# One transpose per score tile with keys in order, and another order of the first tokens, experts and projections

## The chip, the cores and the metric

The kernel runs on one core of a Trainium2 chip. The core has five engines that run side by side: TensorE (PE) for matrix products, VectorE (DVE), ScalarE (ACT), GpSimd (POOL), and SyncE (SP), which here only issues transfers. ACT and POOL issue transfers too. Sixteen DMA engines move the data. The metric is device time in microseconds (us), the median of several executions; one further execution is recorded instruction by instruction, and that record is the profile.

## The reference

The input x is four sequences (batches) of 512 tokens with 256 features, all in float32. Three blocks are added to it in turn:

```
x = x + 0.5 * ffn(layernorm(x))
x = x + attention(layernorm(x))
x = x + 0.5 * ffn(layernorm(x))

ffn(x):       logits = x @ router_w + router_b           # 8 experts
              w = softmax of the two largest logits, 0 for the rest
              h = silu(x @ expert_w[e] + expert_b[e])    # 256 x 256 each
              y = x + (sum over e of w[e] * h[e]) @ proj_w + proj_b
              return norm_w * y / rms(y)

attention(x): 16 query heads, 4 key and value heads, head size 128
              q, k with rotary positions, k scaled by a weight per head
              p = softmax(causal(q k^T / sqrt(128)))
              return concat(p v) @ wo^T
```

## The kernel before

**Tiles.** A batch of 512 tokens is four token tiles of 128. Everything stays in SBUF; weights are loaded once. The first ffn of batches 0 and 1 is computed densely: every token goes through all eight experts (`ffn_dense`, line 683, which calls `ffn_experts`, 303, per token tile and then `ffn_finish`, 514). One step of `ffn_experts` takes a pair of experts: PE multiplies into PSUM (311), DVE adds the bias (316), ACT applies Silu (318), and DVE adds the two weighted results to `acc` (322, 324). The other batches are routed: tokens are gathered by expert into slots, and each slot tile loads its expert's weights from a copy in DRAM (`slots_pair`, 458 to 493, tiles `wt`). The last batches of the last block are dense again. `ffn_route` (217) does layernorm, the transposes of the tokens, the logits and the choice of two experts; in the transposes (`transposed`, 203) ACT copies the first half out of PSUM, and for dense batches DVE copies the second (210).

**Attention.** A group is one batch and one key/value head with its four query heads, so there are 16 groups. `project` (700) computes the group's key and its four queries, each with rotary positions (`rope`, 543). The four token tiles of queries are split into three parts, `PARTS = ((0, 1), (2,), (3,))`, so there are 48 units of a group and a part. `attn_scores` (604) handles a unit. For each query tile t it takes four score tiles r; each has on its 128 partitions 32 query positions times 4 heads, and as columns the (4t + r + 1) × 32 keys that these positions may see. PE computes the scores (615), DVE adds the mask and takes the maximum (617), ACT the exponentials and sums (622), DVE the reciprocals (626), ACT scales (628).

Then the probabilities are turned so that keys lie on partitions. DVE's transpose turns blocks of 32 × 32 where they lie: partitions stay within their quarter of 32. A key index is 128 j + 32 c + i. The tile `turned` has the axes [partition, c, j, x], where x is head-in-quarter and query. Whole key tiles j are written by one transpose (632) that splits the columns into (j, c, i) and writes c outermost; the remaining one to three blocks by a second (637). Sixteen copies by DMA per unit (645), one for each quarter g of partitions and each c, move the block rows to partitions 32 c to 32 c + 31 of `prT`. The blocks that the causal mask leaves out are set to zero once at the start (727). `attn_values` (651) multiplies with v, and `attn_out` (668) with wo.

**Memory that is used twice.** Until attention starts, the three `turned` tiles (`places`, 86) hold the expert weights of the first dense ffn: the first two pairs of experts are in the tile of part 2, the third in that of part 0, the fourth in that of part 1 (`experts`, 93). So a part's scores can't be written before the experts that lie there are done with.

**Order.** The loads are issued at the top of the program on SP's queue, in the order of the lines: batch 0, the four pairs of experts with their biases, batch 1, the attention weights; some small ones on ACT's. An issue waits where the semaphore that it uses belongs to an earlier load that hasn't landed. After the start (lines 718 to 732) a loop over the 48 units runs at 784: it projects a later group's heads, scores unit n + 2, and multiplies unit n by the values; steps of the other ffn work are put between by hand, each at its place (738 to 773). The program text isn't yet the order on the engines: a scheduler with its own estimate of times (line 44) merges what is written into one order for each engine, and an engine then runs its list strictly in order.

Of the kernel before, what the change touches and what calls it, by code (L numbers as in the profile page):

```python
# [9 lines left out]
F32 = mybir.dt.float32  # L10
# [5 lines left out]
P = 128  # L16
B = 4
S = 512
D = 256
H = 16  # L20
KV = 4
G = H // KV
HD = 128
E = 8
# [3 lines left out]
BL = 32  # L28
# [20 lines left out]
def macaron(ctx: ExitStack, tc: tile.TileContext, x, wq, wk, wv, wo, key_weights, router_w, router_b,  # L49
# [26 lines left out]
    def load_x(b):  # L76
        nc.sync.dma_start(xs[b], x[b * S : (b + 1) * S, :].rearrange("(t p) d -> p t d", p=P))

    load_x(0)
    nc.scalar.dma_start(rw, router_w.rearrange("(c p) e -> p c e", p=P))  # L80
    nc.scalar.dma_start(rb, router_b.partition_broadcast(P))
    nc.scalar.dma_start(rmp, ramp.partition_broadcast(P))

    places = [
        const.tile([P, NB, sum(t + 1 for t in ts), G * BL], F32, tag=f"turned{i}", name=f"turned{i}")
        for i, ts in enumerate(PARTS)
    ]

    def experts(who):
        flat = [a.rearrange("p c j x -> p (c j x)") for a in places]
        ews = [
            r.rearrange("p (e c f) -> p e c f", e=2, c=NC)
            for r in (flat[2][:, : 4 * D], flat[2][:, 4 * D :], flat[0][:, : 4 * D], flat[1][:, : 4 * D])
        ]
        eb = work.tile([P, E, D], F32, tag="prT", name=f"eb_{who}")
        for j in range(4):  # L100
            e = 2 * j
            for c in range(NC):
                nc.sync.dma_start(
                    ews[j][:, :, c, :],
                    expert_w[e : e + 2, c * P : (c + 1) * P, :].rearrange("e p f -> p e f"),
                )
            nc.sync.dma_start(
                eb[:, e : e + 2, :].rearrange("p e f -> p (e f)"),
                expert_b[e : e + 2, :].rearrange("e f -> (e f)").partition_broadcast(P),
            )  # L110
        return ews, [eb[:, 2 * j : 2 * j + 2, :] for j in range(E // 2)]

    def experts_late():
# [14 lines left out]
            yield  # L128

    dense = {0: experts(0)}  # L130
    load_x(1)
    nc.scalar.dma_start(pw, proj_w.rearrange("(c p) f -> p c f", p=P))
    nc.scalar.dma_start(pb, proj_b.partition_broadcast(P))
    nc.scalar.dma_start(nw, norm_w.partition_broadcast(P))
# [68 lines left out]
    def transposed(xn, xnT, who, ts=range(NT), dense=False):  # L203
        some = slice(ts[0] * P, (ts[-1] + 1) * P)
        for c in range(NC):
            pt = psum.tile([P, S], F32, tag="pt", name=f"ptx_{who}_{c}")
            for t in ts:
                nc.tensor.transpose(pt[:, t * P : (t + 1) * P], xn[:, t, c * P : (c + 1) * P], ident)
            if c == 1 and dense:
                nc.vector.tensor_copy(xnT[c][:, some], pt[:, some])  # L210
            else:
                nc.scalar.copy(xnT[c][:, some], pt[:, some])
# [4 lines left out]
    def ffn_route(f, b, group=None, ts=range(NT), half=False):  # L217
# [13 lines left out]
                dense_routed[f, b] = xn, xnT, {}  # L231
            xn, xnT, fws = dense_routed[f, b]
        yield from layernorm(b, xn, who, ts)
        transposed(xn, xnT, who, ts, group is None)
        if group:
            rows = slice(k * P, (k + NT) * P)
            nc.gpsimd.dma_start(group.xn[rows, :].rearrange("(t p) d -> p t d", p=P), xn)
# [62 lines left out]
        for i, t in enumerate(ts):  # L300
            fws[t] = fw[:, i, :]

    def ffn_experts(f, b, t, routed, weights):
        _, xnT, fws = routed
        ews, ebs = weights
        who = f"f{f}_{b}_{t}"
        acc = work.tile([P, 2, D], F32, tag="ga", name=f"acc_{who}")[:, 0, :]
        for j in range(E // 2):
            ph = psum.tile([P, 2, D], F32, tag="sc", name=f"ph_{who}_{j}", bufs=3)
            for c in range(NC):  # L310
                nc.tensor.matmul(  # L311
                    ph, xnT[c][:, t * P : (t + 1) * P], ews[j][:, :, c, :],
                    start=(c == 0), stop=(c == NC - 1),
                )
            h = work.tile([P, 2, D], F32, tag="h", name=f"h_{who}_{j}")
            nc.vector.tensor_tensor(h, ph, ebs[j], ALU.add)  # L316
            s = work.tile([P, 2, D], F32, tag="tb", name=f"s_{who}_{j}", bufs=3)
            nc.scalar.activation(s, h, AF.Silu)  # L318
            for i in range(2):
                e = 2 * j + i  # L320
                if e == 0:
                    nc.vector.tensor_scalar_mul(acc, s[:, i, :], fws[t][:, 0:1])
                else:
                    nc.vector.scalar_tensor_tensor(acc, s[:, i, :], fws[t][:, e : e + 1], acc, ALU.mult, ALU.add)
        return acc
# [277 lines left out]

    def attn_scores(ts, part, qT, kT, who):
        turned = places[part]
        runs = sum(t + 1 for t in ts)
        first = 0
        for t in ts:
            nm = small.tile([P, NB], F32, tag="nm", name=f"nm_{who}_{t}")
            sums = small.tile([P, NB], F32, tag="sums", name=f"sums_{who}_{t}")  # L610
            prs = []
            for r in range(NB):
                n = (NB * t + r + 1) * BL
                ps = psum.tile([P, S], F32, tag="sc", name=f"ps_{who}_{t}_{r}", bufs=3)
                nc.tensor.matmul(ps[:, :n], qT[:, NB * t + r, :, :], kT[:, :n], start=True, stop=True)  # L615

                nc.vector.tensor_tensor_reduce(  # L617
                    out=ps[:, :n], in0=ps[:, :n], in1=mask[:, S - n :], scale=-1.0, scalar=-LOWEST,
                    op0=ALU.add, op1=ALU.min, accum_out=nm[:, r : r + 1],
                )  # L620
                pr = work.tile([P, S], F32, tag="pr", name=f"pr_{who}_{t}_{r}", bufs=5)
                nc.scalar.activation(  # L622
                    pr[:, :n], ps[:, :n], AF.Exp, bias=nm[:, r : r + 1], scale=-1.0, accum_out=sums[:, r : r + 1]
                )
                prs.append((n, pr))
            nc.vector.reciprocal(sums, sums)  # L626
            for r, (n, pr) in enumerate(prs):
                nc.scalar.mul(pr[:, :n], pr[:, :n], sums[:, r : r + 1])  # L628

                whole = n // P  # L630
                if whole:
                    nc.vector.transpose(  # L632
                        turned[:, :, first : first + whole, r * BL : (r + 1) * BL].rearrange("p c j q -> p j c q"),
                        pr[:, : whole * P].rearrange("p (j c i) -> p j c i", c=NB, i=BL),
                    )
                if whole * P < n:
                    nc.vector.transpose(
                        turned[:, : r + 1, first + t, r * BL : (r + 1) * BL],
                        pr[:, whole * P : n].rearrange("p (c i) -> p c i", i=BL),
                    )  # L640
            first += t + 1
        prT = work.tile([P, NB, NT * G * BL], F32, tag="prT", name=f"prT_{who}")
        for g in range(NB):
            for c in range(NB):
                nc.sync.dma_start(  # L645
                    prT[c * BL : (c + 1) * BL, g, : runs * P],
                    turned[g * BL : (g + 1) * BL, c, :, :].rearrange("p j x -> p (j x)"),
                )
        return prT

# [61 lines left out]
    def score(n):  # L712
        if n < len(units):
            g, ts = units[n]
            who = "_".join(str(i) for i in (*groups[g], ts[0]))
            prTs[n] = attn_scores(ts, PARTS.index(ts), qTs[g], kTs[g], who)

    dense_routed = {}
    at_once(ffn_route(0, 0))
    ffn_dense(0, 0, dense[0], ffn_route(0, 1))  # L720
    ffn_dense(0, 1, dense[0], attn_prepare(0))

    for turned, ts in zip(places, PARTS):
        first = 0
        for t in ts:
            for c in range(1, NB):
                nc.gpsimd.memset(turned[:, c, first + t, : c * BL], 0.0)
            first += t + 1
    project(0, range(G))
    score(0)  # L730
    project(1, (0, 1))
    score(1)


    PLACES = 4
# [116 lines left out]
```

## Time and profile before

| | us |
|---|---|
| median of three runs | 888.08 |
| lowest and highest run | 885.06 and 888.1 |
| the profiled execution | 882.37 |
| its span, first to last instruction | 880.7 |

The span is what the profile's times are measured in; the profiled execution is 1.7 us longer than its span. The profile's first page gives each engine's busy time. The chain that ended last is followed back from the last instruction, at each step to what released it, so its shares say what the end of the program hung on. A row of a timeline reads: start, length, engine, line, operation, what is written and read, how many instructions are merged, and in brackets how long the engine was idle before and what ended that. "SPq" and "ACTq" are the queues on which an engine issues transfers. The granted clock is the share of TensorE's full speed.

### The profile page before, as it was taken

To read this page: it belongs to the slowest core of one execution; us is meant where nothing else is said; L and a number is where in the kernel's file an instruction comes from. 1 tells how busy PE (TensorE), PEld (TensorE's weight loads), DVE (VectorE), ACT (ScalarE), POOL (GpSimd) and SP (SyncE) were. 2 spreads that over 40 slices of the span, in tenths; PEclk is the share of its full clock that TensorE was granted. 3 is DMA by queue.
4 is the path that set the end of the run, shared out by engine and by line. 5 is a ranking of instruction groups with operands and counts; after the bars stand their busy time and mean duration, and the time that the engine had idled before them with its cause. 6 is when DMAs were issued, how large, how long until landed. Compare 5 with 4: busy or idle time off the path is not lost.

```text
span 880.7 us, 11501 instructions
## 1 busy us (share of the span) xinstructions
PE 807.2 (92%) x2752; PEld 478.4 (54%) x2752; DVE 624.1 (71%) x1961; ACT 512.4 (58%) x1260; POOL 301.0 (34%) x402
## 2 busy tenths in 40 slices
PE   4899798999999898999989999999799979999995
PEld 2444344656466555565545556657566546645552
DVE  1889569786357677776387878447674788788795
ACT  1444359656547574686487766647664576673263
POOL 4123274213142217672312322242322765301222
PEclk9999999899999999999999999999999999999997
DMA  7900011335576655243213333466666334342000
GB/s 237 409 24 6 20 60 43 85 81 142 139 224 188 193 145 152 69 118 107 61 34 87 98 106 89 135 181 199 196 175 211 88 112 135 108 118 74 13 7 24
DMA packets 68979, 103.32 MB, mean 117 GB/s; under 512 B 16624, under 2 KB 47600, under 8 KB 68528
## 3 DMA queue, kind: packets, MB, share of 16 engines
q1 hardware_dynamic: 61744, 84.48, 32.5%
q0 software_dynamic: 6048, 17.57, 7.1%
q10 hardware_dynamic: 1120, 0.54, 0.2%
q8 instruction: 22, 0.36, 0.2%
q14 instruction: 45, 0.37, 0.1%
HBM read 45.11 MB, written 15.47 MB: 69 GB/s over the span
## 4 chain that ended last, share of the span: by engine, by line
PE 53%; SPq 13%; DVE 11%; DMA 9%; ACT 9%; issue 4%; POOL 1%; POOLq 0%; ACTq 0%; DVEq 0%
SPq L645 12%; PE pa L658 10%; PE pw L671 8%; PE ph_f L311 7%; PE pp_q L584 6%; PE ps L615 6%; DMA wt<-wb 3%; PE ph_f L337 3%; PE phg L485 3%; PE po_f L524 3%; ACT tb_q L553 3%; PE pp_k L584 2%; ACT pr L622 2%; PE pv_a L573 2%; ACT pr L628 2%
## 5 line engine op out<-in xcount | busy, mean ns | idle before, releaser
L622 ACT ACTIVATE pr<-ps,nm 128x32 f32<-128x32 f32 (+15 forms) x256 | 123.2, 485 | 76.6 <-DVE nm L617 66.2
L615 PE MATMUL ps<-kT,qT 128*128 128x160 f32 (+15 forms) x512 | 146.9, 408 | 13.0 <-ACT pr L622 12.5
L658 PE MATMUL pa<-prT,v_a 128*128 128x512 f32 x320 | 149.8, 596 | 2.8 <-DMA prT<-turned 1.1
L617 DVE CUSTOM_DVE_ANT_0 ps<-ps,mask 128x32 f32<-128x32 f32 (+15 forms) x256 | 110.5, 446 | 40.5 <-PE ps L615 38.8
L560 POOL TENSOR_TENSOR qT<-qT,tb_q 128x512 f32<-128x512 f32 x64 | 81.2, 1271 | 156.2 <-DVE tb_q L558 101.7
L584 PE MATMUL pp_q<-xnT_a,wq_sb 128*128 128x512 f32 x256 | 124.2, 615 | 4.4 <-DVE qT L557 1.8
L615 PEld LDWEIGHTS ps<-kT,qT 128*128 128x128 f32 x512 | 86.6, 191 | 69.5 <-issue 32.4
L671 PE MATMUL pw<-wo_sb,oT 128*128 128x256 f32 x512 | 122.0, 382 | 1.8 <-ACT oT L664 1.1
L628 ACT ACTIVATE pr<-pr,sums 128x32 f32<-128x32 f32 (+15 forms) x256 | 112.3, 511 | 12.7 <-DVE sums L626 12.2
L671 PEld LDWEIGHTS pw<-wo_sb,oT 128*128 128x128 f32 x512 | 96.9, 191 | 31.1 <-issue 13.3
L553 ACT ACTIVATE tb_q<-pp_q,kws 64x512 f32<-64x512 f32 x128 | 87.4, 683 | 30.8 <-PE pp_q L584 28.8
L632 DVE STREAM_TRANSPOSE turned<-pr 128x128 f32<-128x128 f32 (+3 forms) x208 | 93.1, 447 | 16.8 <-ACT pr L628 14.4
L658 PEld LDWEIGHTS pa<-prT,v_a 128*128 128x128 f32 x320 | 58.6, 190 | 58.4 <-issue 54.1
L584 PEld LDWEIGHTS pp_q<-xnT_a,wq_sb 128*128 128x128 f32 x256 | 48.6, 196 | 56.1 <-issue 44.5
L469 POOL DMA_INDIRECT xg<-xn_dram,source x46 | 44.9, 976 | 92.8 <-PE ptg L477 64.0
L557 DVE SCALAR_TENSOR_TENSOR qT<-pp_q,kws,cos_sb 128x512 f32<-128x512 f32 x64 | 47.8, 748 | 33.2 <-ACT tb_q L553 32.6
L311 PE MATMUL ph_f<-turned,xn_f 128*128 128x512 f32 x128 | 64.0, 652 | 5.3 <-DVE h_f L316 5.3
L664 ACT COPY oT<-pa 128x512 f32<-128x512 f32 x64 | 37.1, 580 | 32.4 <-PE pa L658 29.9
L318 ACT ACTIVATE s_f<-h_f 128x512 f32<-128x512 f32 x48 | 29.6, 628 | 43.8 <-DVE h_f L316 28.1
L558 DVE TENSOR_TENSOR tb_q<-tb_q,sin_sb 128x512 f32<-128x512 f32 x64 | 52.1, 815 | 0.3 <-ACT tb_q L553 0.3
L485 PE MATMUL phg<-wt,xT 128*128 128x256 f32 x184 | 46.0, 383 | 6.4 <-DMA wt<-wb 6.4
L622 ACT ACTIVATION_READ_ACCUMULATOR pr<-ps,nm 128x1 f32 x256 | 50.2, 196 | 0.0
(168 smaller groups left out, 1165.7 us busy)
## 6 DMA issues: line engine op xcount, KB each, us to landing
prT<-turned SPq DMA_DIRECT2D x512, 48.0 KB
wt<-wb SPq DMA_DIRECT2D x46, 384.0 KB
prT<-turned SPq DMA_DIRECT2D x256, 64.0 KB
rows<-hg SPq DMA_DIRECT2D x22, 256.0 KB
x<-in_x_dram SPq DMA_DIRECT2D x4, 512.0 KB
turned<-in_expert_w_dram SPq DMA_DIRECT2D x8, 256.0 KB
wq_sb<-in_wq_dram SPq DMA_DIRECT2D x1, 2048.0 KB
wo_sb<-in_wo_dram SPq DMA_DIRECT2D x1, 2048.0 KB
```

The source lines that it names most:

```text
L311: nc.tensor.matmul(ph, xnT[c][:, t * P : (t + 1) * P], ews[j][:, :, c, :], start=(c == 0), stop=(c == NC - 1),)
L553: nc.scalar.mul(tb[o, :], ps[i, :], scale[i, :])
L560: nc.gpsimd.tensor_tensor(dst, dst, blocks(tb), ALU.subtract)
L584: nc.tensor.matmul(ps, w[:, c, h * HD : (h + 1) * HD], xnT[:, c, :], start=(c == 0), stop=(c == NC - 1))
L615: nc.tensor.matmul(ps[:, :n], qT[:, NB * t + r, :, :], kT[:, :n], start=True, stop=True)
L617: nc.vector.tensor_tensor_reduce(out=ps[:, :n], in0=ps[:, :n], in1=mask[:, S - n :], scale=-1.0, scalar=-LOWEST, op0=ALU.add, op1=ALU.min, ...
L622: nc.scalar.activation(pr[:, :n], ps[:, :n], AF.Exp, bias=nm[:, r : r + 1], scale=-1.0, accum_out=sums[:, r : r + 1])
L628: nc.scalar.mul(pr[:, :n], pr[:, :n], sums[:, r : r + 1])
L632: nc.vector.transpose(turned[:, :, first : first + whole, r * BL : (r + 1) * BL].rearrange("p c j q -> p j c q"), pr[:, : whole * P].rearr ...
L645: nc.sync.dma_start(prT[c * BL : (c + 1) * BL, g, : runs * P], turned[g * BL : (g + 1) * BL, c, :, :].rearrange("p j x -> p (j x)"),)
L658: nc.tensor.matmul(po, v[:, j, kv * HD : (kv + 1) * HD], prT[:, :, (first + j) * P : (first + j + 1) * P], start=(j == 0), stop=(j == t),)
L671: nc.tensor.matmul(pw_, oT[:, i, :], wo_sb[:, kv * G + i, :], start=(i == 0), stop=(i == G - 1))
```

## The change

There are three edits.

1. `turned` now has the axes [partition, key block, x], with key block 4 j + c, in the order of the keys. Each score tile is turned by one transpose whatever its number of blocks. The copies take every fourth key block.
2. The first token tile of batch 0 is loaded and routed alone. The rest of batch 0 and batch 1 are loaded behind the first pair of experts, ahead of the other three pairs.
3. The dense ffn of batch 1 is written out: tiles 0 and 1 as before, the pairs of experts of tiles 2 and 3 in the order 2, 3, 0, 1, and between them batch 0's attention preparation and its first projections. The zeros of part 0 come before the first scores, the other parts' after them; the finish of tiles 2 and 3 stands behind the first scores and the first head of the second group.

Besides, in the last block the second half of the tokens' transposes is copied by ACT, as the first half is, and no longer by DVE.

```diff
-    load_x(0)
+    nc.sync.dma_start(xs[0][:, 0, :], x[:P, :])
...
-        const.tile([P, NB, sum(t + 1 for t in ts), G * BL], F32, tag=f"turned{i}", name=f"turned{i}")
+        const.tile([P, NB * sum(t + 1 for t in ts), G * BL], F32, tag=f"turned{i}", name=f"turned{i}")
...
+            if j == 0:
+                nc.sync.dma_start(xs[0][:, 1:, :], x[P:S, :].rearrange("(t p) d -> p t d", p=P))
+                load_x(1)
...
-    load_x(1)
...
-        transposed(xn, xnT, who, ts, group is None)
+        transposed(xn, xnT, who, ts, group is None and f == 0)
...
-                whole = n // P
-                if whole:
-                    nc.vector.transpose(
-                        turned[:, :, first : first + whole, r * BL : (r + 1) * BL].rearrange("p c j q -> p j c q"),
-                        pr[:, : whole * P].rearrange("p (j c i) -> p j c i", c=NB, i=BL),
-                    )
-                if whole * P < n:
-                    nc.vector.transpose(
-                        turned[:, : r + 1, first + t, r * BL : (r + 1) * BL],
-                        pr[:, whole * P : n].rearrange("p (c i) -> p c i", i=BL),
-                    )
+                nc.vector.transpose(
+                    turned[:, first : first + n // BL, r * BL : (r + 1) * BL],
+                    pr[:, :n].rearrange("p (k i) -> p k i", i=BL),
+                )
...
-                    prT[c * BL : (c + 1) * BL, g, : runs * P],
-                    turned[g * BL : (g + 1) * BL, c, :, :].rearrange("p j x -> p (j x)"),
+                    prT[c * BL : (c + 1) * BL, g, : runs * BL].rearrange("p (j x) -> p j x", x=G * BL),
+                    turned[g * BL : (g + 1) * BL, c:runs:NB, :],
...
-    at_once(ffn_route(0, 0))
+    at_once(ffn_route(0, 0, ts=(0,)))
+    at_once(ffn_route(0, 0, ts=(1, 2, 3)))
     ffn_dense(0, 0, dense[0], ffn_route(0, 1))
-    ffn_dense(0, 1, dense[0], attn_prepare(0))
...
+    acc0 = experts_of(0)
+    acc1 = experts_of(1)
+    finish(0, acc0)
+    at_once(attn_prepare(0))
+    acc2 = experts_of(2, (2, 3))
+    finish(1, acc1)
+    acc3 = experts_of(3, (2, 3))
+    project(0, (0,))
+    acc2 = experts_of(2, (0,), acc2)
+    project(0, (1,))
+    acc3 = experts_of(3, (0,), acc3)
+    project(0, (2,))
+    acc2 = experts_of(2, (1,), acc2)
+    project(0, (3,))
+    acc3 = experts_of(3, (1,), acc3)
+    zeros(0)
     score(0)
-    project(1, (0, 1))
+    finish(2, acc2)
+    project(1, (0,))
+    finish(3, acc3)
+    project(1, (1,))
+    zeros(1)
+    zeros(2)
     score(1)
```

Here `experts_of(t, pairs, acc)` is `ffn_experts` for batch 1, tile t, which now takes a list of pairs and a sum to go on from; `finish` is `ffn_finish` for that batch, and `zeros(part)` does the memsets of one part.

More of the change, by code (lines that the diff above doesn't have):

```diff
@@ L93, in experts @@
     def experts(who):
[L94 to L98, printed above, removed]
+        room = [places[2][:, :8, :], places[2][:, 8:, :], places[0][:, :8, :], places[1][:, :8, :]]
+        ews = [r.rearrange("p (e c h) x -> p e c (h x)", e=2, c=NC) for r in room]
         eb = work.tile([P, E, D], F32, tag="prT", name=f"eb_{who}")
@@ L301, in ffn_route, with ffn_experts @@
             fws[t] = fw[:, i, :]
-    def ffn_experts(f, b, t, routed, weights):
+    def ffn_experts(f, b, t, routed, weights, pairs=range(E // 2), acc=None):
         _, xnT, fws = routed
@@ L306, in ffn_experts @@
         who = f"f{f}_{b}_{t}"
-        acc = work.tile([P, 2, D], F32, tag="ga", name=f"acc_{who}")[:, 0, :]
-        for j in range(E // 2):
+        first = acc is None
+        if first:
+            acc = work.tile([P, 2, D], F32, tag="ga", name=f"acc_{who}")[:, 0, :]
+        for j in pairs:
             ph = psum.tile([P, 2, D], F32, tag="sc", name=f"ph_{who}_{j}", bufs=3)
@@ L320, in ffn_experts @@
                 e = 2 * j + i
-                if e == 0:
-                    nc.vector.tensor_scalar_mul(acc, s[:, i, :], fws[t][:, 0:1])
+                if first and e == 2 * pairs[0]:
+                    nc.vector.tensor_scalar_mul(acc, s[:, i, :], fws[t][:, e : e + 1])
                 else:
@@ L605, in attn_scores @@
         turned = places[part]
-        runs = sum(t + 1 for t in ts)
+        runs = NB * sum(t + 1 for t in ts)
         first = 0
@@ L628, in attn_scores @@
                 nc.scalar.mul(pr[:, :n], pr[:, :n], sums[:, r : r + 1])
-                whole = n // P
-                if whole:
-                    nc.vector.transpose(
-                        turned[:, :, first : first + whole, r * BL : (r + 1) * BL].rearrange("p c j q -> p j c q"),
-                        pr[:, : whole * P].rearrange("p (j c i) -> p j c i", c=NB, i=BL),
-                    )
-                if whole * P < n:
-                    nc.vector.transpose(
-                        turned[:, : r + 1, first + t, r * BL : (r + 1) * BL],
-                        pr[:, whole * P : n].rearrange("p (c i) -> p c i", i=BL),
-                    )
-            first += t + 1
+                nc.vector.transpose(
+                    turned[:, first : first + n // BL, r * BL : (r + 1) * BL],
+                    pr[:, :n].rearrange("p (k i) -> p k i", i=BL),
+                )
+            first += NB * (t + 1)
         prT = work.tile([P, NB, NT * G * BL], F32, tag="prT", name=f"prT_{who}")
@@ L718, in macaron, with experts_of, finish, zeros @@
     dense_routed = {}
-    at_once(ffn_route(0, 0))
+    at_once(ffn_route(0, 0, ts=(0,)))
+    at_once(ffn_route(0, 0, ts=(1, 2, 3)))
     ffn_dense(0, 0, dense[0], ffn_route(0, 1))
-    ffn_dense(0, 1, dense[0], attn_prepare(0))
-    for turned, ts in zip(places, PARTS):
+    routed = dense_routed.pop((0, 1))
+    def experts_of(t, pairs=range(E // 2), acc=None):
+        return ffn_experts(0, 1, t, routed, dense[0], pairs, acc)
+    def finish(t, acc):
+        at_once(ffn_finish(0, 1, t, routed[0][:, t, :], acc))
+    def zeros(part):
         first = 0
-        for t in ts:
+        for t in PARTS[part]:
             for c in range(1, NB):
-                nc.gpsimd.memset(turned[:, c, first + t, : c * BL], 0.0)
-            first += t + 1
-    project(0, range(G))
-    score(0)
-    project(1, (0, 1))
+                nc.gpsimd.memset(places[part][:, first + NB * t + c, : c * BL], 0.0)
+            first += NB * (t + 1)
+    acc0 = experts_of(0)
[14 more added lines that the diff above has]
+    zeros(0)
+    score(0)
+    finish(2, acc2)
[4 more added lines that the diff above has]
+    zeros(2)
     score(1)
```

## The prediction

> **What bounds the kernel now.** I read the first page (busy shares, the chain that ended last), then the time cut by stage, then what TensorE (PE) waits for, then the queue of SyncE (SP), because the chain names it.
>
> ```profile
> PE 807.2 (92%) x2752; PEld 478.4 (54%) x2752; DVE 624.1 (71%) x1961; ACT 512.4 (58%) x1260; POOL 301.0 (34%) x402
> PE 53%; SPq 13%; DVE 11%; DMA 9%; ACT 9%; issue 4%; POOL 1%; POOLq 0%; ACTq 0%; DVEq 0%
> ```
>
> PE carries the time, but the second owner of the chain is not VectorE (DVE): it is SP's queue, and nearly all of that (12% by line) is the issuing of the copies of line 645.
>
> ```profile
> 0.00:25.00 25.00, 11.47 (x38) 6.50 (x39) 6.53 (x25) 3.71 (x4) 9.36 (x37) 1.00 0.77 258
> 25.00:60.00 35.00, 34.59 (x99) 17.19 (x98) 31.21 (x95) 17.31 (x30) 7.59 (x13) 0.90 0.61 237
> 60.00:100.00 40.00, 37.78 (x104) 18.22 (x103) 28.58 (x76) 14.09 (x31) 10.45 (x22) 0.96 0.04 14
> 100.00:110.00 10.00, 4.12 (x15) 2.69 (x14) 7.46 (x18) 3.64 (x8) 3.71 (x7) 0.86 0.00 0
> 110.00:160.00 50.00, 44.24 (x134) 23.50 (x133) 40.28 (x122) 35.27 (x84) 28.38 (x34) 0.88 0.18 54
> 160.00:810.00 650.00, 616.31 (x2188) 378.58 (x2187) 456.08 (x1469) 410.68 (x1052) 224.38 (x258) 0.99 0.46 130
> ```
>
> Columns: stretch, length, busy PE, weight loads, DVE, ScalarE (ACT), POOL, then granted clock, DMA share, GB/s. Before 160 us PE is idle 27.8 us and its clock is below 1; in the 650 us after that it is idle 33.7 us at full clock. The start is where time lies loose. Two waits hold most of it:
>
> ```profile
> 22.35 1.08 DVE L192 BATCH_NORM_STATS2 st_f<-x 128x6 f32<-128x256 f32 x3 [10.63 <-DMA x<-in_x_dram]
> 24.46 5.83 PE L311 MATMUL ph_f<-turned,xn_f 128*128 128x512 f32 x9 [4.06 <-DVE h_f L316]
> 108.09 0.66 PE L518 MATMUL ptc_f<-ident,acc_f 128*128 128x128 f32 x2 [5.88 <-DVE acc_f L324]
> ```
>
> DVE stands 10.63 us before the statistics of batch 1, whose load comes last, and PE stands behind it. At 108 us PE waits 5.88 us for the last token tile's sum, with the projections queued behind. In the main stage, SP's queue:
>
> ```profile
> 454.67 90.90 SPq L645 DMA_DIRECT2D prT<-turned  x135
> L645 SPq DMA_DIRECT2D prT<-turned x768: 507/589/1952, 147.9 to 806.6; - x192
> L77 SPq DMA_DIRECT2D x<-in_x_dram x4: 368/406/449, 1.5 to 22.3; - x4
> L538 SPq DMA_DIRECT2D out_dram<-x x8: 332/332/519, 807.2 to 877.6; - x8
> L493 SPq DMA_DIRECT2D rows<-hg x24: 338/385/1460, 241.0 to 674.6; - x24
> ```
>
> 135 issues without a break in 90.9 us are 0.673 us each; the median issue is 0.589, and about 0.045 passes between two (the 16 of one unit, from 281.56, took 10.78 with one slow one of 1.31). So 0.634 is SP's floor, 10.15 us per unit of 16, and the units pass every 10.77. Between 460 and 540 us PE is busy 76.85 of 80, 10.3 us per unit: PE and SP are bound together there.
>
> **The change, part by part. (a) Transposes.** Their rows:
>
> ```profile
> L632 DVE STREAM_TRANSPOSE turned<-pr 128x384 f32<-128x384 f32 x64 | 35.7, 558 | 6.2 <-ACT pr L628 4.4 <-DMA prT<-turned 1.7
> L632 DVE STREAM_TRANSPOSE turned<-pr 128x256 f32<-128x256 f32 x64 | 27.5, 430 | 5.9 <-ACT pr L628 5.4 <-DMA prT<-turned 0.3
> L632 DVE STREAM_TRANSPOSE turned<-pr 128x128 f32<-128x128 f32 x64 | 19.0, 297 | 4.6 <-ACT pr L628 4.5
> L637 DVE STREAM_TRANSPOSE turned<-pr 128x96 f32<-128x96 f32 x64 | 15.5, 242 | 0.1
> L637 DVE STREAM_TRANSPOSE turned<-pr 128x64 f32<-128x64 f32 x64 | 13.5, 211 | 0.3
> L637 DVE STREAM_TRANSPOSE turned<-pr 128x32 f32<-128x32 f32 x64 | 11.5, 179 | 3.1 <-ACT pr L628 2.5 <-DMA prT<-turned 0.4
> ```
>
> 128 columns more cost 128 to 133 ns, so a fixed part of 150 to 170 ns stands in every instruction. Each score tile of the query tiles 1 to 3 whose keys don't fill whole tiles has two transposes: 3 × 3 × 16 groups = 144 pairs become one. 144 × 0.15 = 21.6 us off DVE. DVE isn't the bound: it holds 11% of the chain, 97 us, out of 624 busy; the same share of 21.6 is 3.4 us. I take −3.5; 0 if PE and SP cover it all, −8 if also the ps and pr handshake shortens (PE waits 9.2 us on ACT's pr in the main stage). The new form's stride is only longer; where it costs more per column than 1 ns no row shows, and a twentieth more on 134 us of transposes would be 6 us of DVE, under 1 on the chain.
>
> **(b) The copies of line 645.** Their number stays 768. The source of each was one run of 1.5 or 2 KB per partition; now it is three or four runs of 512 B, 96 or 128 pieces instead of 32. Nothing in this trace issues a copy from SBUF to SBUF in such pieces, so I bound it. Rows: 128 rows in one run each take 0.332 to issue (out), 256 pieces 0.385 (rows), 512 pieces 0.406 (x): more pieces and one dimension more cost 0.05 to 0.075. Lower end 0. The other end: the present copy already takes 0.257 more than out with a quarter of the rows, for a reason the trace doesn't show; if a dimension more costs that again, +0.257. I take +0.06, from the nearest count of pieces. SP's floor becomes 0.694, 11.1 us per unit. The stretches that SP fills without a break (from 159.99: 77 issues in 51.01; 454.67: 135 in 90.90; 720.39: 80 in 52.92; 775.50: 37 in 24.68) hold 20.6 units at 10.67. (11.1 − 10.67) × 20.6 = +9. The chain says the same: 12.4% of 880.7 is 109 us, 172 issues × 0.06 = +10. I take +9, from 0 to about +110 (below). What waits behind SP: the next unit's copies, the expert rows wt that PE waits for (6.4 us now), and so pa. On the 16 DMA engines the copies move the same 42 MB; their share is 0.46 in that stage, and I cost them at nothing; without that cover, 0.2 us more to landing on some ten copies that stand on the chain would be 2.
>
> A rule speaks against this part. The Trainium skill, Perfetto Trace Analysis, section What "DMA-bound" means, says that the window of an issuing sequencer is descriptor generation, and that large descriptors are what matter. If issue time went with the number of pieces, an issue would take 1.8 to 2.4 us and the stage would more than double; the rows above (512 pieces in 0.406) don't show that, so the rule moves no term here.
>
> **(c) First loads.** Now batch 1 lands behind 0.5 (batch 0) + 2 (weights) + 1 (biases) MB and ACT's 0.5, at 22.3 us. After the change only 0.13 + 0.77 + 0.38 MB of SP's stand before its 0.5, with ACT's 0.5 some 2.3 MB. The first 10 us move 1.67 MB, the next 10 go at 277 GB/s: about 12.3 us. The price: the other three pairs of experts wait behind 0.5 MB more, 1.8 us, the last landing near 20.6. DVE's stop is gone; late next are the weights. By 24.46 PE has done three expert steps (one step is four matmul records, 1.72 us in the chain). After, with token tile 0 finished at 22.3, it has done 5.2, that is 3.9 us gained; steps of other tiles drawn forward make 6.4 at most. Lower end 0: ACT issues pw, pb and nw, and each issue waits for an earlier load (at 3.03, 5.21, 7.39 now). If nw waits for batch 1, ACT's first copy goes from 10.81 to about 14. I take −4.5. The first tile routed alone adds some 15 small DVE instructions of 0.15 to 0.2 and at most two table loads of 1.28: 5.5 us, hidden by DVE's 6.5 busy of 25; uncovered they eat the gain.
>
> **(d) Experts between projections.** From 60 to 160 us PE is idle 13.9 us. The work doesn't shrink, it is put into these gaps: the 5.88 at 108 and half of the other 8 go. Next to bind is DVE: 76 us busy of these 100, 76 of 93 after. I take −7 (0 to −12). POOL's memsets now stand ahead of each score stage instead of in a block; 12 × 0.12 = 1.4 us, hidden by POOL's idle 7 of 10. The end of the dense stage, finish of tiles 2 and 3, is moved behind the first scores; only batch 0's own last steps need it.
>
> **(e) Clock.** (1 − 0.90) × 35 + 0.04 × 40 + 0.14 × 10 + 0.12 × 50 = 12.5 us of the start are lost to a lower clock, after the gaps. Two gaps fewer: −2 (0 to −4).
>
> **(f) The last block's copies from DVE to ACT:** three, 1 us, where DVE is busy 54 of the last 70: −0.5; ACT has room.
>
> Sum: −3.5 + 9 − 4.5 − 7 − 2 − 0.5 = −8.5. The profiled execution took 882.37 us (span 880.7, 1.7 around it): 873.9. The median of the runs is 888.08, 5.7 above; carried over, 879.6, said as 879.
>
> **Rivals.** *SP takes over* (slower). The 17.5 us of gains are used up when a unit takes 0.85 more on 20.6 units: 11.52 us, 0.72 per issue with its gap, so from +0.086 per issue on it is slower. At +0.15, (12.54 − 10.67) × 20.6 = 38, less 17.5: +21, 909. At +0.257, 14.26 a unit: +74, and in the 260 us with expert slots (some 18 units of 14 us) +2 each: 980. For it: the unbroken queue. Against it: the flat rows of issue time. *The start gives nothing*: DVE, busy 31.2 of 35 from 25 to 60, or ACT's queue becomes the bound there. −4 + 9 = +5: 893. For it: how full DVE is; against: 28 us of PE idle. *The copies cost SP nothing*: −17.5, with more from the start up to −28: 860 to 870.
>
> **How the numbers follow.** This forecast (own range 869 to 886) 0.47; SP takes over 0.23; the start gives nothing 0.15; copies free 0.15. Half a per cent, 4.4 us, is what a measurement can tell from no change. Faster: 0.82 of the forecast, all of the free case: 0.53. Same: 0.15, the rest of the forecast and part of the idle start. Slower 0.32. 864 to 912 leaves out the low tail of the free case and SP beyond +0.15, together under 2 in 10.
>
> **What would show it.** The issue of line 645: median 0.64 to 0.66 confirms (b), above 0.68 (0.72 with the gap) ends the forecast. 256 transposes, about 112 us. Batch 1's statistics near 12 us; no PE wait of several us near 108; PE idle before 160 near 15. It goes wrong if the order in which the engines get the new work puts a late load ahead of ready work, or SP's queue shows breaks, which would mean it was never the bound.

## The result, and the profile after

The changed kernel is slower: 890.2 us median (886.17 to 895.14) against 885.37 (878.92 to 889.11) for before on the same chip, a ratio of 1.0061 with a 95% interval of 1.0042 to 1.0081. The forecast of 879 us, 9 below the 888.08 that stood for before, went the wrong way, though the time lies within its range. The profiled execution took 888.89 us, its span 887.2, 6.5 more than that of before's profile.

The first page of the changed kernel, busy times and the chain by engine:

```profile
PE 807.6 (91%) x2752; PEld 480.2 (54%) x2752; DVE 626.2 (71%) x1833; ACT 515.6 (58%) x1268; POOL 304.1 (34%) x404
PE 51%; SPq 14%; DVE 14%; DMA 8%; ACT 7%; issue 4%; POOL 1%; POOLq 0%; DVEq 0%; ACTq 0%
```

The same stretches as in the prediction (length, busy PE, weight loads, DVE, ACT, POOL, then granted clock, DMA share, GB/s), of the changed kernel:

```profile
0.00:25.00 25.00, 14.63 (x41) 7.67 (x42) 12.39 (x56) 7.87 (x10) 11.51 (x42) 0.93 0.79 269
25.00:60.00 35.00, 33.02 (x108) 17.41 (x106) 29.33 (x92) 16.67 (x31) 8.32 (x14) 1.00 0.59 229
60.00:100.00 40.00, 39.43 (x100) 18.52 (x101) 32.51 (x80) 15.93 (x31) 13.07 (x24) 0.96 0.04 14
100.00:110.00 10.00, 5.82 (x15) 2.67 (x14) 8.55 (x14) 6.36 (x10) 3.72 (x3) 0.94 0.00 0
110.00:160.00 50.00, 43.14 (x155) 26.42 (x155) 41.66 (x142) 36.79 (x98) 26.91 (x39) 0.87 0.24 69
160.00:810.00 650.00, 606.53 (x2138) 372.75 (x2137) 443.92 (x1290) 402.37 (x1029) 223.43 (x252) 0.98 0.47 128
```

Before 160 us PE is idle 24.0 us instead of 27.8. In the 650 us after that it is idle 43.5 instead of 33.7, and the clock is a hundredth lower. So the start did gain, and the main stage lost more. Where the start's waits stood (start, length, engine, line, and in brackets the idle time before), batch 1's statistics and PE's wait near 108 us:

```profile
13.11 1.08 DVE L191 BATCH_NORM_STATS2 st_f<-x 128x6 f32<-128x256 f32 x3 [4.29 <-DMA x<-in_x_dram]
14.99 1.08 DVE L191 BATCH_NORM_STATS2 st_f<-x 128x6 f32<-128x256 f32 x3 [0.58 <-DMA x<-in_x_dram]
...
107.68 0.44 PE L519 MATMUL ptc_f<-ident,acc_f 128*128 128x128 f32 x2 [3.18 <-DVE acc_f L325]
```

DVE's stop of 10.63 us is now 4.29 (for the rest of batch 0) and 0.58; the 5.88 us at 108 are 3.18. The transposes (count, then busy time in us and mean in ns, then DVE's idle time before them) and the issue of the copies (count, then shortest/median/longest in ns, first and last start in us):

```profile
L630 DVE STREAM_TRANSPOSE turned<-pr 128x32 f32<-128x32 f32 (+15 forms) x256 | 108.7, 447 | 14.9 <-ACT pr L629 11.5
...
L638 SPq DMA_DIRECT2D prT<-turned x768: 305/598/1963, 135.3 to 810.5; - x192
```

The median issue grew by 9 ns, from 589 to 598, not by 60. The first copy is issued at 135.3 us, 12.6 earlier than before (147.9); the last at 810.5, 3.9 later (806.6). From first to last copy the main stage takes 675.2 us where before takes 658.7: 16.5 us are lost there. What loses them is the question of the experiments.

### The profile page after: what moved, and what is told of

Same layout as the page of the kernel before. It is cut to its first block, busy times and chain, and to the rows that moved or that the text cites. A ratio compares the mean times of both kernels' runs of the same rounds, so it can differ in the third digit from the quotient of the medians.

```text
span 887.2 us, 11351 instructions
## 1 busy us (share of the span) xinstructions
PE 807.6 (91%) x2752; PEld 480.2 (54%) x2752; DVE 626.2 (71%) x1833; ACT 515.6 (58%) x1268; POOL 304.1 (34%) x404
## 2 busy tenths in 40 slices
DMA packets 126338, 103.31 MB, mean 116 GB/s; under 512 B 16640, under 2 KB 113152, under 8 KB 125888
## 4 chain that ended last, share of the span: by engine, by line
PE 51%; SPq 14%; DVE 14%; DMA 8%; ACT 7%; issue 4%; POOL 1%; POOLq 0%; DVEq 0%; ACTq 0%
SPq L638 13%; PE pa L651 9%; PE pw L664 8%; PE ph_f L312 7%; PE pp_q L585 7%; PE ps L616 6%; PE ph_f L338 3%; PE phg L486 3%; DMA wt<-wb 3%; DVE ps L618 2%; PE po_f L525 2%; PE pv_a L574 2%; PE pp_k L585 2%; ACT pr L623 2%; DVE acc_f L325 2%
## 5 line engine op out<-in xcount | busy, mean ns | idle before, releaser
L616 PEld LDWEIGHTS ps<-kT,qT 128*128 128x128 f32 x512 | 89.0, 195 | 65.5 <-issue 34.6
L630 DVE STREAM_TRANSPOSE turned<-pr 128x32 f32<-128x32 f32 (+15 forms) x256 | 108.7, 447 | 14.9 <-ACT pr L629 11.5
L486 PE MATMUL phg<-wt,xT 128*128 128x256 f32 x184 | 48.3, 396 | 10.6 <-DMA wt<-wb 10.2
L559 DVE TENSOR_TENSOR tb_q<-tb_q,sin_sb 128x512 f32<-128x512 f32 x64 | 54.0, 844 | 0.0
```

What stands on the lines that cost most here:

```text
L630: nc.vector.transpose(turned[:, first : first + n // BL, r * BL : (r + 1) * BL], pr[:, :n].rearrange("p (k i) -> p k i", i=BL),)
```

## The experiments

**Parts alone and undone.** The first four take the edits apart. One kernel has only the new start; against the changed kernel its layout is the old one again, with copies in one run and two transposes (two of its places):

```diff
-        const.tile([P, NB * sum(t + 1 for t in ts), G * BL], F32, tag=f"turned{i}", name=f"turned{i}")
+        const.tile([P, NB, sum(t + 1 for t in ts), G * BL], F32, tag=f"turned{i}", name=f"turned{i}")
...
-                    turned[g * BL : (g + 1) * BL, c:runs:NB, :],
+                    turned[g * BL : (g + 1) * BL, c, :, :].rearrange("p j x -> p (j x)"),
```

> The changed kernel with the old layout of the turned tiles and the old two transposes and contiguous copies; the new order of loads, first tokens, experts and projections, and the ACT copies of the last block, stay. Theory SP: in the changed kernel the first unit's copies start 12.6 us earlier, and that lead is lost because each of the 768 copies takes 9 ns longer to issue (about 0.15 us per unit) and because a late queue then makes two stalls near 645 and 786 us. With the old copies back, the lead of about 10 us stays: 874 to 879 us, ratio to the kernel before 0.988 to 0.993. Rival A, the lead is borrowed: work was only pushed from the start into the main stage, so it is given back there anyway: ratio 0.998 to 1.003. Rival B, chance of the merged order: the stalls come with any new order, ratio anywhere from 0.99 to 1.006, with a lead of 10 us at the first units and a sudden loss of 5 us or more later.

Its counterpart is before with the layout alone, by the same lines the other way round.

> The kernel before with the new layout, the single transpose per score tile and the strided copies alone. Theory SP: DVE's 25 us saved are worth nothing, the copies cost 768 x 0.009 = 7 us of a full queue and some knock-on: ratio 1.004 to 1.012, the issue at 0.598. The prediction's term for DVE (3.5 us saved) with the measured issue time would give a ratio of 0.996 to 1.003.

The third is the changed kernel with each score tile cut into whole key tiles and the rest again, and the copies left strided:

```diff
-                nc.vector.transpose(
-                    turned[:, first : first + n // BL, r * BL : (r + 1) * BL],
-                    pr[:, :n].rearrange("p (k i) -> p k i", i=BL),
-                )
+                cuts = [c for c in (0, n // P * P, n) if c <= n]
+                for lo, hi in zip(cuts, cuts[1:]):
+                    if lo < hi:
+                        nc.vector.transpose(
+                            turned[:, first + lo // BL : first + hi // BL, r * BL : (r + 1) * BL],
+                            pr[:, lo:hi].rearrange("p (k i) -> p k i", i=BL),
+                        )
```

> The changed kernel with its new layout and strided copies, but each score tile turned by two transposes, whole key tiles and the rest, as before. Theory SP: DVE stands beside a full SP queue, so putting its 22 to 25 us back costs 0 to 2 us: ratio to the kernel before 1.004 to 1.010, as the changed kernel's 1.006. If DVE's saving carried the change, it costs 3.5 to 8 us: ratio 1.010 to 1.016.

The fourth relieves SP of a quarter of the copies:

```diff
-                nc.sync.dma_start(
+                (nc.gpsimd if g == 3 else nc.sync).dma_start(
```

> The changed kernel with 4 of the 16 copies of a unit (those of the last quarter of partitions) issued by POOL instead of SP. Theory SP: SP's floor falls from 10.3 to 7.7 us per unit, so the units with little other work pass at PE's pace of about 10.3 and the lead from the start stays: ratio 0.980 to 0.994. If SP's full queue only mirrors PE's pace, nothing is won and POOL's 192 issues of about 0.63 us (121 us on POOL, whose list is in order and must wait for DVE's transposes) delay the rotary positions: ratio 1.006 to 1.03.

Measured: the new start alone 0.9942 (0.9921 to 0.9963), the layout alone 1.0164 (1.0122 to 1.0207), the changed kernel with two transposes 1.0046 (1.0022 to 1.0069), with POOL issuing a quarter 1.0131 (1.0106 to 1.0157). The new start alone lies in the range of the rival of the merged order, the two transposes in that of SP's queue, POOL's quarter in that of the rival that SP only mirrors PE's pace; the layout alone lies outside both of its ranges. The last run doesn't support SP as the bound, since with a quarter of its issues gone the kernel got slower still; it doesn't rule it out either, since POOL's busy time rose from 304.1 to 413.3 us, and PE then waited 8.7 us for `pa` (the product with the values) behind `oT` and 8.4 behind the copies. But the layout alone costs 14 us, far more than 768 issues of 9 ns, 6.9 us, can explain. Something else than the issue of the copies is in these numbers.

**The two halves of the start.** Two more kernels split the start: one has only the new loads and the first token tile routed alone, the other only the experts between the projections.

```diff
-    load_x(0)
+    nc.sync.dma_start(xs[0][:, 0, :], x[:P, :])
...
-    at_once(ffn_route(0, 0))
+    at_once(ffn_route(0, 0, ts=(0,)))
+    at_once(ffn_route(0, 0, ts=(1, 2, 3)))
```

> Before, with the new order of the first loads and the first token tile routed alone; nothing else. The start's share of the gain that holds: by the forecast's term 0.5% (4.5 us), 0.994 to 0.996. If what is gained ahead of 60 us is lost at 108 us or later, 0.999 to 1.001. If the first half of the start's gain is all there is, as much as the whole order change: 0.993.

```diff
-    ffn_dense(0, 1, dense[0], attn_prepare(0))
+    acc0 = experts_of(0)
+    acc1 = experts_of(1)
+    finish(0, acc0)
+    at_once(attn_prepare(0))
+    acc2 = experts_of(2, (2, 3))
...
```

> Before, with the experts of the last token tiles put between the first projections and the finishes behind the first scores; loads, first token tile and layout as before. By the forecast's term 0.8% (7 us and 1 of clock): 0.990 to 0.993. If it is lost again in the merged order of the main stage: 0.997 to 1.003.

Measured: the loads alone 1.0161 (1.0133 to 1.0190), the experts alone 1.0035 (1.0014 to 1.0057). Both expectations missed, and the parts don't add: each half alone is slower than before, the two together (0.9942) faster. The trace of the loads' kernel has its first copy at 145.8 us, 2.1 earlier than before, and its last at 817.8, 11.2 later; nothing of what it changed runs at that time. The time goes in units whose work this edit doesn't touch.

What all these kernels have in common is that the planner (the scheduler that merges the program into one order for each engine) merged their program anew. Set side by side with before, by runs of instructions that match, 1271 to 1358 of PE's 1505 instructions keep their order in the kernels with a part alone, 1280 in the changed one. So the merged order became the rival cause.

**The same instructions in another order.** To test it I took the order of all engines from one kernel and imposed it on another, instruction by instruction, with edges that order the lists and bring no wait of their own. Where one kernel has two transposes and the other a single one, the single one takes the place of the later of the two. Before, given its own order in this way, is the same program.

```diff
+    traced = {i.name: i for i in nc.cur_bb.bb.instructions}
...
+        for earlier, later in zip(names, names[1:]):
+            tc.add_manual_dep(
+                traced[later], earlier,
+                mybir.DependencyInfo(mybir.DependencyClass.NoSync, mybir.DependencyReason.DATA), reason="given order",
+            )
```

The first pair crosses copies and order: both have two transposes and the new start.

> The kernel with the new layout and the strided copies but two transposes, every engine held to the merged order of the kernel with the old layout (which took 0.9942 of before). Only the pieces of the copies (512 B for 1536 and 2048) differ from that kernel. If the copies themselves cost the time (SP's queue: 768 issues by 9 ns more is 7 us at most, and their landing), it is 1.002 to 1.006, like the kernel with two transposes in its own order. If the order in which the engines got the work costs it, 0.992 to 0.997.

> The other way round: the old layout and its copies in one run per partition, every engine held to the merged order of the kernel with strided copies and two transposes (1.0046 of before). If the copies themselves cost the time, it is 0.991 to 0.996, like the old layout in its own order. If the order costs it, 1.002 to 1.007.

| | order of the old layout's kernel | order of the strided kernel |
|---|---|---|
| copies in one run | 0.9942 (0.9921 to 0.9963) | 0.9977 (0.9954 to 1.0000) |
| copies in 512-byte pieces | 0.9988 (0.9964 to 1.0012) | 1.0046 (1.0022 to 1.0069) |

Neither theory has it alone: the copies cost 0.0046 and 0.0069, the order 0.0035 and 0.0058. Each difference is uncertain by about 0.003, as two intervals enter it; the 0.0035 is the least sure, its two intervals overlap. The next four are again held to the order of another kernel.

> The changed kernel, whole (single transposes, strided copies, new start), with every engine held to the merged order of the kernel with the old layout and the new start (0.9942 of before). If about half of the loss was the order (the four runs so far put the copies at +0.005 to +0.007 and the order at +0.004 to +0.006), this is 0.995 to 0.999: the copies' price without the order's, less whatever 25 us of VectorE are worth. If the single transposes in their own right cost the time, it stays at 1.004 to 1.008.

> Before, with the new layout alone (single transposes, strided copies), every engine held to before's merged order. In an order of its own this was 1.0164. If the copies cost 0.5% and the order the rest: 1.002 to 1.007. If the layout itself costs it: 1.013 to 1.020. If VectorE's 25 us count once nothing else moves: 0.995 to 1.000.

> Before, with the new first loads and first token tile alone, held to before's merged order from the third unit on. In its own order it was 1.0161 although its first copies were issued 2.1 us earlier. If the order cost it: 0.996 to 0.999, the 2 us of lead kept. If the new loads themselves make something late afterwards: 1.010 to 1.018.

> Before, with the experts between the first projections alone, held to before's merged order from the third unit on. In its own order it was 1.0035 although its first copies were issued 9.4 us earlier. If the order ate the lead: 0.988 to 0.992. If a lead at the start is lost in any order, because a later load or queue sets the pace: 0.997 to 1.003.

Measured: the changed kernel in the order of the old layout with the new start 0.9995 (0.9971 to 1.0018), where its own gave 1.0061. The layout alone in before's order 1.0036 (1.0012 to 1.0060), where its own gave 1.0164. The loads alone 0.9990 (0.9966 to 1.0013), where their own order gave 1.0161; their lead (how much earlier than before the first copies are issued) had shrunk to 0.7 us, and this is the weak end of what was expected of them. With the order held, the large unexplained losses of these three are gone. The experts alone stayed at 1.0027 (1.0003 to 1.0050): the held part began so early that the first `pa` came at 164.2 us, 1.7 later than before's, though the first copies were issued at 133.0. The lead was lost at that border, so this run decides nothing.

**Before's order, from the tenth unit on.** With the border, the unit from which the order is held, moved back, the first nine units are free and nothing of the start is bent.

> The old layout with the whole new start, every engine held to before's merged order from the tenth unit on (the border is put there so that the first units are free). In its own order this start gave 0.9942; its lead of 11 us at the first copies was 9 until the 34th unit and gone at the 37th, then about 2 to 4. If the order of the late units ate the lead: 0.987 to 0.991. If in any order something that comes late there (expert rows, the second group's slots) takes the lead back: 0.993 to 0.998.

> The changed kernel, whole, held to before's merged order from the tenth unit on. If the order is what made it slower: the start's 0.987 to 0.991 and the copies' 0.004 to 0.006 give 0.992 to 0.997, below before. If the layout costs more than the start brings: 1.000 to 1.005. In its own order 1.0061, in that of the old layout with the new start 0.9995.

> Before, with the experts between the first projections alone, held to before's merged order from the tenth unit on. With the border at the third unit the lead was lost at the border itself (the copies of the first unit came 15 us earlier, the first pa 1.7 us later). If order is all: the lead of 9 us stays, 0.988 to 0.992. If a lead at the start is lost later in any order: 0.997 to 1.004, as in its own order (1.0035).

Measured: the new start with the old layout 0.9900 (0.9876 to 0.9923), the whole change 0.9930 (0.9905 to 0.9955), the experts alone 0.9949 (0.9928 to 0.9970), between their two ranges: half of their lead stayed. The whole change, the same instructions as in the slower kernel, is now 0.7% faster than before instead of 0.6% slower. The issue of its copies and its chain:

```profile
L766 SPq DMA_DIRECT2D prT<-turned x768: 585/598/1794, 134.5 to 796.9; - x192
...
PE 54%; DVE 13%; ACT 10%; DMA 8%; SPq 7%; issue 4%; POOL 3%; POOLq 0%; DVEq 0%; ACTq 0%
```

The issue is the same 598 ns and starts at nearly the same time, 134.5 for 135.3. But the last copy is issued at 796.9, not at 810.5, and SP's share of the chain is 7%, half of the changed kernel's. First to last copy in the kernels that ran both ways, from the starts that their issue rows give (the layout alone is held throughout, the loads alone from the third unit, the others from the tenth):

| kernel | in its own order, us | held to before's order, us |
|---|---|---|
| before | 147.9 to 806.6: 658.7 | |
| new start, old layout | 136.6 to 805.4: 668.8 | 134.9 to 796.0: 661.1 |
| changed kernel | 135.3 to 810.5: 675.2 | 134.5 to 796.9: 662.4 |
| its two transposes back | 135.2 to 818.0: 682.8 | 136.4 to 806.5: 670.1 |
| layout alone | 145.2 to 819.8: 674.6 | 146.3 to 812.8: 666.5 |
| loads alone | 145.8 to 817.8: 672.0 | 147.2 to 807.8: 660.6 |
| experts alone | 138.5 to 807.5: 669.0 | 137.6 to 800.3: 662.7 |

All six orders that the planner made for edited programs take 10 to 24 us longer in this stage than the one it made for before; in before's order the same programs take 2 to 11 longer. Not in the table is the experts alone held from the third unit, whose lead went at the border: 133.0 to 813.3, 680.3 us.

**What is left: the transposes, and the place.** Two last kernels: the changed one with two transposes in before's order, and the changed one whole, held only from the thirtieth unit on.

> The changed kernel with the strided copies but two transposes again, held to before's merged order from the tenth unit on. The same held order with the old layout gave 0.990, with the whole change 0.993. If the single transposes' 19 us of VectorE are worth something once the order stands, this is 0.995 to 0.998 (copies without that gain). If they are worth nothing: 0.992 to 0.994, and the copies alone are the 0.003.

> The changed kernel, whole, in its own order up to the 30th unit and held to before's order from there on. Its own order lost about 14 us against the held one between the first and the last copy: 4 by the 29th unit, 10 after it. If the order of the late units is where the loss sits: 0.994 to 0.998. If the loss comes from an earlier state (a lead that is already spoilt), 1.001 to 1.006.

Measured: 0.9959 (0.9939 to 0.9979) and 0.9951 (0.9934 to 0.9969). Under one order, then, the strided copies cost 0.0059 (0.9900 to 0.9959) and the single transposes give back 0.0029 (0.9959 to 0.9930), with overlapping intervals. An earlier pair doesn't repeat that gain: in the order of the old layout's kernel the strided copies took 0.9988 with two transposes and 0.9995 with one. So the gain is not settled. The layout as a whole, copies and single transposes together, costs 0.0030 (0.9900 to 0.9930), 0.0036 (alone, in before's order) and 0.0053 (0.9942 to 0.9995) under three given orders.

Nor does SP's share of the chain follow the order or the time. With the two transposes back it is 6% in the planner's order, where the kernel took 1.0046 of before, and 10% in before's, where it took 0.9959:

```profile
PE 54%; DVE 15%; ACT 8%; DMA 8%; SPq 6%; issue 6%; POOL 3%; POOLq 0%; DVEq 0%; ACTq 0%
PE 51%; DVE 14%; SPq 10%; DMA 9%; ACT 8%; issue 5%; POOL 3%; POOLq 0%; DVEq 0%; ACTq 0%
```

And holding the late units alone brings 1.0061 to 0.9951: 1.1 of the 1.3% between the two orders sits in the last nineteen of the 48 units.

There one can see it happen. SP's queue and PE's slot matmuls `phg` in the changed kernel, from its rows by time:

```profile
627.40 9.28 SPq L638 DMA_DIRECT2D prT<-turned  x12
637.21 0.73 SPq L468 DMA_DIRECT2D wt<-wb  x2
638.02 0.38 SPq L494 DMA_DIRECT2D rows<-hg  x1
638.63 1.48 SPq L468 DMA_DIRECT2D wt<-wb  x2
640.21 0.61 SPq L494 DMA_DIRECT2D rows<-hg  x1
642.63 11.28 SPq L638 DMA_DIRECT2D prT<-turned  x16
...
629.88 1.89 PE L486 MATMUL phg<-wt,xT 128*128 128x256 f32 x8
643.35 1.13 PE L486 MATMUL phg<-wt,xT 128*128 128x256 f32 x4 [3.31 <-DMA wt<-wb]
```

The same in the changed kernel with before's order:

```profile
620.16 11.84 SPq L766 DMA_DIRECT2D prT<-turned  x16
632.25 0.98 SPq L596 DMA_DIRECT2D wt<-wb  x2
633.34 0.38 SPq L622 DMA_DIRECT2D rows<-hg  x1
633.95 1.15 SPq L596 DMA_DIRECT2D wt<-wb  x2
635.21 0.82 SPq L622 DMA_DIRECT2D rows<-hg  x1
...
638.49 1.03 PE L614 MATMUL phg<-wt,xT 128*128 128x256 f32 x4
639.78 1.03 PE L614 MATMUL phg<-wt,xT 128*128 128x256 f32 x4
```

In both, the four loads of expert rows `wt` stand behind a unit's copies. In the planner's order PE's list has `phg` next and PE stands 3.31 us until the rows land (the chain shows 6.10 us for that load). In before's order the loads are issued just as late behind the copies, and PE's list has other work until they have landed: no `phg` row from there to the stretch's end at 653 us shows a stop. The sum for the stretch (columns as above), changed kernel in its own order:

```profile
600.00:810.00 210.00, 187.96 (x636) 113.61 (x635) 151.31 (x408) 125.41 (x323) 77.41 (x92) 0.96 0.49 136
```

and in before's:

```profile
600.00:810.00 210.00, 195.80 (x670) 118.64 (x669) 153.43 (x423) 123.65 (x317) 76.56 (x94) 0.98 0.47 132
```

PE is idle 22.0 us in the one and 14.2 in the other, and its clock is 0.96 against 0.98; before itself has 14.7 and 0.99 there. The changed kernel's longest single waits of PE there are 3.6 us (`pp_k`, for DVE's `qT`), 3.3 (`phg`, shown) and 2.2 (`pa`, for the copies); in before's order the same three are 1.6, 1.5 and 0.6 at their longest, and the longest of all is 2.7, for ACT's `pr` (1.4 in the changed kernel). It is a handful of stops in different places, not one.

## Why the prediction was wrong, by its own steps

**The step that failed is the sum itself.** It took 8.5 us from the end of the program for terms that were each worked out where they arise, in the order of before, and so took for granted that the merged order of the rest stays. It didn't: the planner gave the later units another order, which cost about 13 us between first and last copy (675.2 against 662.4) and made −0.7% into +0.6%. The prediction named this at its end ("the order in which the engines get the new work puts a late load ahead of ready work") but looked for it in the new work, gave it no price and made it none of the rivals. With before's order held, the whole change took 872.72 us when profiled, and the sum had said 873.9; that closeness is luck. The profiled execution is near the fastest of its eight (872.14 to 880.18), the ratio 0.9930 is a gain of 6.2 us and not 8.5, and two misses in it cancel in part: the start gave 8.8 us for 14, and the layout cost 2.6 for 5.5.

**(a) Transposes, −3.5 of 0 to −8.** 256 by 447 ns are 114 us, forecast 112: 19 us off the transposes. DVE's busy time as a whole didn't fall with them in the planner's order (624.1 us before, 626.2 after); in before's order it is 629.3 with two transposes and 622.1 with one. What they are worth in time is 2.6 us in one pair and nothing in the other, both without clear intervals: within the bounds, but the 3.5 isn't shown.

**(b) Copies, +9 of 0 to +110.** The issue took 0.009 us more, not 0.06; 0.598 refutes the forecast's 0.64 to 0.66. Yet the copies cost 0.0046, 0.0069 and 0.0059 in three pairs, 4 to 6 us. All 768 issues together grew by 6.9 us, so most of them would have to stand on the path for that to be the whole cause. Where a page gives the median time from issue to landing, it is 1.9 and 2.0 us for copies of 48 and 64 KB in one run (the loads alone) and 2.0 and 2.1 in pieces (the changed kernel in the order of the old layout), one execution each; what share that has wasn't separated. The Trainium skill (Perfetto Trace Analysis, What "DMA-bound" means) says that where the issuing sequencer binds, large descriptors are what matter. The issue time doesn't bear that out for these copies: three to four times the pieces, 1.5% more of it. The term's premise, that PE and SP are bound together and SP's 13% of the chain can be priced by the issue, failed too: with 598 ns per issue that share was 14, 10, 7 and 6% in four kernels, and it fell from 14 to 7 in the same program by another order alone.

**(c) Loads, −4.5.** Alone they brought the first copies 2.1 us forward. Batch 1's statistics ran at 14.99, not near 12; the expert weights became late next, as the prediction said (PE waited 2.42 us for them before 15.69). As a lead that is half of what was taken, within its bounds; in time the loads alone gave nothing clear of noise, 0.9990 with before's order held.

**(d) Experts between projections, −7.** Alone they brought the first copies 9.4 us forward, and with the order held 4.5 us stayed (0.9949), within the bounds of 0 to −12. The wait at 108 us was to vanish and is 3.18; PE's idle time before 160 us was to be near 15 and is 24.0.

**(e) Clock, −2.** By the same working, 12.5 us lost in before's start are now 10.5 (0.93, 1.00, 0.96, 0.94 and 0.87 in the five stretches), and 8.3 in the whole change with before's order held (1.00, 1.00, 0.96, 0.88 and 0.89): −2 and −4, in one execution each. **(f)** wasn't run by itself.

(c) to (f) were to give 14 us; with the old layout and before's order they gave 0.0100, 8.8 us, and 9.9 in the profiled spans.

**The rivals.** "SP takes over" had the right sign and the wrong mechanism: its threshold was +0.086 per issue, and the issue grew by a tenth of that. "The start gives nothing" is refuted by the 0.9900. "The copies cost SP nothing" is nearest for SP's queue and wrong for the copies, which do cost.

## What to carry to other kernels

Where a planner merges the program, an edit is two changes: what was written, and a new order for everything behind it, which here moved the time of the whole change by 1.3%, and that of the loads alone, which touch none of the later units, by 1.7%. Test an edit with the old order imposed on the rest, and judge it by that; a comparison between two planned orders, even of a few lines, measures both. Here that also gave a version faster than both kernels: the new start with the old layout, in before's order from the tenth unit on, 0.9900 of before.

## What the runs showed of the hardware that was not expected

A copy within SBUF in three or four 512-byte pieces per partition row instead of one of 1.5 or 2 KB, 126338 packets in all instead of 68979, took 598 ns to issue instead of 589, and the DMA engines were busy 0.47 of the main stage instead of 0.46. Why before's own merged order is better than all six others is not shown by any of these runs.
